# A wait ahead of the first weight load, finer evictions of one block, and an adapter product moved two matmuls ahead, in a fused low-rank-adapter and FFN kernel

## Chip, core and metric

The kernel runs on one core of one Trainium2 chip. The metric is device time in microseconds (us). TensorE is called PE, its weight load PEld, VectorE DVE, ScalarE ACT, GpSimd POOL, and SyncE SP; SP issues most of the DMAs. Code lines are written L424.

## What is computed

The input x has 8 sequences of 256 tokens and 1024 features. Each sequence picks one of 8 adapters of rank 16; the result goes through a gated FFN whose three inputs are rounded to fp8, and is added to x:

```
Bx   = einsum('bni,bri->bnr', x, B[ids])        # rank 16
c    = einsum('bnr,bor->bno', Bx, A[ids])       # 1024 features
q(v) = clip(v / in_scale, -448, 448) to fp8, times in_scale
h    = silu(q(c) @ gate.T) * (q(c) @ up.T)      # 2752 features
out  = x + q(h) @ down.T
```

## The kernel before

All tensors are held transposed: features on the 128 partitions, tokens along the free dimension. The 2048 tokens are four **blocks** t of 512 (two sequences each), the 1024 features eight pieces k of 128, and the 2752 hidden features 22 **chunks** c of 128 (the last has 64). One product is a 128x128 weight tile (bf16, the upper halves of f32 words) times a 128x512 tile of fp8 activations.

*Block 0.* SP loads block 0 of x in four pieces (`PIECES`, L46: k 0 to 1, 2 to 4, 5 to 6, 7; L432, L433, L441, L442), the adapters' B (`b_two`) and A (`a_two`), and then the gate and up weights of chunks 0 to 4 (`load_gate_up`, L418; 1 MB a chunk; chunks 0 and 1 in two halves; L445, L446). All these stand in one SP queue in program order. PE first runs 16 products of ones (`warm`, L750) that only pass time, then `two_times_b` (L553): the tile `bx`, B times x, over k 0 to 7, with two more passing products after k 6. DVE and ACT copy `bx` to `bm`; after six more passing products, `two_times_a` (L618) multiplies by A into `c` tiles, and `round_two` (L610) evicts them: scaled, rounded to fp8, into `xg[0]`, half on DVE (L606) and half on ACT (L608). Each eviction takes one k (256 columns, "singly") or two (512 columns).

*Chunks.* `gate_up(c, t)` (L677) makes 16 products, a gate sum over eight k and an up sum over eight k; `turns` tells in which order the two sums alternate, and `between` runs a function ahead of a given step. Then ACT does the silu (L695) and DVE multiplies and rounds into `hid` (L724). `wpool` holds five weight chunks, so chunk 5's load waits until PE is done with chunk 0. Instructions marked `keep_in_program_order` and all products stay in the order of the code.

*Block 1.* Block 0 runs through chunks 0 to 6 (`NHELD` is 7). Inside chunk 6, ahead of step 4, `two_times_b_in_parts` (L577) makes block 1's `bx`; ahead of step 10, `two_times_a_part(…, 0)` (L654) makes k 0 to 3 of `xg[1]`; and inside chunk 2 of block 1 (L794), ahead of step 5, `two_times_a_part(…, 1)` makes k 4 to 7. Block 1's x (`xs[1]`, 1.75 MB and 0.25 MB) is loaded by SP between the two halves of chunk 6's weights (L770). POOL doubles and splits the adapters for it, after its 1x1 copy at L756, which waits for chunk 2's weights.

*Blocks 2 and 3.* After chunks 3 and 4 of block 1, `four_times_b` (L797) makes `bx` for both blocks. Four groups of A follow, two k each (`four_times_a`, L667; 0 to 3): one inside chunk 5 of block 1, one after it, one inside chunk 6 ahead of step 8, one after it (L798 to L801). Each group has 16 products into four `c` tiles, then two evictions on ACT and two on DVE. Then blocks 2 and 3 pass chunks 2 to 6, and all blocks the rest; the down product (`yd`) and the addition of x (L847) end the kernel.

Of the kernel before, what the change touches and what calls it, by code (L numbers as in the profile page):

```python
# [34 lines left out]
NAHEAD = 2  # L35
NHELD = NFIRST + NAHEAD
# [17 lines left out]
def rows_of(c):  # L54
    return TAIL if c == NI - 1 else P


def high(ap):

    return ap.bitcast(BF16)[..., 1::2]  # L60
# [34 lines left out]
def gate_up_of(w_gu, c):  # L95
    at = c * 2 * NH * P * P
    return w_gu[at : at + 2 * NH * P * rows_of(c)].rearrange("(p n) -> p n", p=P)
# [204 lines left out]
def adaln_ffn(  # L302
# [15 lines left out]
    nc = tc.nc  # L318
# [45 lines left out]
    with ExitStack() as fast:  # L364
# [5 lines left out]
        xs = [acts.tile([P, NH, TB], F32, name=f"x{t}") for t in range(NTB)]  # L370
# [17 lines left out]
        def adapter_of(batch, queue):  # L388
            return queue.value_load(ids_i[0:1, batch : batch + 1], min_val=0, max_val=7)
# [25 lines left out]

        w_of = {}

        def load_gate_up(c, parts=1, between=()):  # L418
            n = NH if c == NI - 1 else 2 * NH
            w = wpool.tile([P, 2 * NH, P], F32, tag="w", name="w_gu")[:, :n]  # L420
            src = gate_up_of(w_gu, c).rearrange("p (k n) -> p k n", n=P)
            n //= parts
            for i in range(parts):
                nc.sync.dma_start(out=w[:, bass.ts(i, n)], in_=src[:, bass.ts(i, n)])  # L424
                if i == 0:
                    for load in between:
                        load()
            w_of[c] = w
# [14 lines left out]
        load_a_two(1, second)  # L443
        load_a_two(0, adapter_of(0, nc.sync))
        for c in range(NFIRST):  # L445
            load_gate_up(c, parts=2 if c < 2 else 1)  # L446
        adapters = [adapter_of(2 + q, nc.gpsimd if q < 2 else nc.sync) for q in range(6)]
        lane = const.tile([P, 1], I32, name="lane")
        nc.gpsimd.iota(lane, pattern=[[0, 1]], base=0, channel_multiplier=1)
# [153 lines left out]
        def round_to(to, c, engine):  # L603
            scale = inv[:, GATE_IN : GATE_IN + 1]
            if engine is nc.vector:
                nc.vector.tensor_scalar(to, c, scale, None, ALU.mult, saturate=False)  # L606
            else:
                nc.scalar.activation(to, c, AF.Copy, scale=scale, saturate=False)  # L608

        def round_two(t, part, cs, cut=False):  # L610
            for g in range(2):
                n = 1 if cut and g == 0 else 2
                for i, j in product(range(0, 2, n), range(2)):
                    k = KS * part + 2 * g + i
                    to = xg[t][:, k : k + n, bass.ts(j, SEQ)]
                    round_to(to, cs[2 * g + j][:, i : i + n], nc.vector if j else nc.scalar)

        def two_times_a(bm):  # L618


            n = SEQ // 2
            for part in range(2):
                cs = [psum.tile([P, 2, SEQ], F32, tag="ps", name=f"c{q}") for q in range(4)]
                for other, i in product(range(2), range(2)):
                    for q in (0, 2, 1, 3):
                        rows = slice(32 * q, 32 * (q + 1))
                        multiply(
                            cs[q][:, i, bass.ts(q % 2 ^ other, n)],
                            lhsT=a_two[0][rows, bass.ts(2 * part + i, P)],
                            rhs=bm[rows, other],  # L630
                            start=True,
                            stop=True,
                        )
                cs = [cs[2 * j + g] for g in range(2) for j in range(2)]
                round_two(0, part, cs, cut=part == 0)

        def times_a_parts(bms, a, at):

            cs = [psum.tile([P, 2, SEQ], F32, tag="ps", name=f"c{q}") for q in range(4)]
            for bm, i in product(bms, range(2)):
                for q in range(4):
                    rows = slice(32 * q, 32 * (q + 1))
                    multiply(
                        cs[q][:, i],
                        lhsT=a[rows, bass.ts(at + i, P)],
                        rhs=bm[rows],
                        start=bm is bms[0] and i == 0,
                        stop=bm is bms[-1] and i == 1,  # L650
                    )
            return cs

        def two_times_a_part(bms, part):  # L654
            round_two(1, part, times_a_parts(bms, a_parts[0], 2 * part), cut=True)

        def four_times_b():
            quads = [(q, 0, 2 + q // 2, bass.ts(q % 2, SEQ)) for q in range(4)]
# [8 lines left out]
        def four_times_a(bms, i):  # L667
            cs = times_a_parts(bms, a_parts[1 + i // 2], 2 * (i % 2))
            for q in range(4):
                to = xg[2 + q // 2][:, 2 * i : 2 * i + 2, bass.ts(q % 2, SEQ)]  # L670
                round_to(to, cs[q], nc.vector if q % 2 else nc.scalar)
# [5 lines left out]
        def gate_up(c, t, turns=(NH,), between={}):  # L677


            tail = c == NI - 1  # L680
            w = w_of[c]
            cols = bass.ts(t, TB)
            js = range(1 if tail else 2)
            ys = []
            steps = []
            for i, n in enumerate(turns):
                done = sum(turns[:i])
                steps += product(js, range(done, done + n))
            rows = slice(TAIL, P) if tail else slice(0, P)
            g = work.tile([P, TB], F32, tag="g", name="g")  # L690

            def silu():
                gates = ys[0][:TAIL] if tail else ys[0]
                early(
                    nc.scalar.activation(  # L695
                        g[rows], gates, AF.Silu, scale=gate_s[: gates.shape[0]]
                    )
                )

            def early(instruction):  # L700
                if c < NHELD:
                    tc.keep_in_program_order(instruction)

            for i, (j, k) in enumerate(steps):
                if i in between:
                    between[i]()
                if j == len(ys):
                    ys.append(psum.tile([P, TB], F32, tag="ps", name=f"y{j}"))
                multiply(
                    ys[j],  # L710
                    lhsT=high(w[:, row_of(c, j, k), :]),
                    rhs=xg[t][:, k, :],
                    start=(k == 0),
                    stop=(k == NH - 1),
                )
                if j == 0 and k == NH - 1:
                    silu()
            ups = ys[0][TAIL:] if tail else ys[1]
            if tail:
                to = lora.tile([P, 2 * TB], FP8, tag="bm", name="tail", bufs=2)[half_of(t), :TB]  # L720
            else:
                to = hid_of(c)[:, cols]
            early(
                nc.vector.scalar_tensor_tensor(  # L724
                    to,
                    in0=ups,
                    scalar=up_by_down[rows],
                    in1=g[rows],
                    op0=ALU.mult,
                    op1=ALU.mult,  # L730
                    saturate=False,
                )
            )
            if tail:
                nc.vector.tensor_copy(hid_tail[half_of(t), t // 2], to)
            if t == (NTB - 1 if NAHEAD <= c < NHELD else 2 if c < NAHEAD else 1):
                note_low_bits(w_of[c], P, c)
                if 1 < c <= 1 + 2 * NTB:
                    i, half = divmod(c - 2, 2)
                    ks = slice(half * NH // 2, (half + 1) * NH // 2)  # L740
                    note_squares(xg[i][:, ks, :], P, c - 2)
                before = NHELD - 1 if c == 0 else NAHEAD - 1 if c == NHELD else c - 1
                if c != NAHEAD:
                    note_squares(hid[before], P, 2 * NTB + before)
# [14 lines left out]
        for g, j in product(range(2), range(2)):  # L759
            load_a_twice(a_two[1], 2 * g + j, a8_twice, adapters[j] * 2 + g, nc.gpsimd)  # L760
        a_parts = [
            in_place_of_hid(NI - 8 - i, [P, H // 2], F32R, f"a_parts{i}") for i in range(3)
        ]
# [19 lines left out]
        for c in range(2, NHELD - 1):  # L783
            gate_up(c, 0)
        bms = []
# [3 lines left out]
            between={  # L789
                4: lambda: bms.append(two_times_b_in_parts()),  # L790
                10: lambda: two_times_a_part(bms[0], 0),
            },
        )
        gate_up(NAHEAD, 1, turns=(4, 1, 1, 2), between={5: lambda: two_times_a_part(bms[0], 1)})  # L794
        for c in range(NAHEAD + 1, NHELD - 2):
            gate_up(c, 1)
        bms.append(four_times_b())  # L797
        gate_up(NHELD - 2, 1, between={8: lambda: four_times_a(bms[1], 0)})  # L798
        four_times_a(bms[1], 1)
        gate_up(NHELD - 1, 1, between={8: lambda: four_times_a(bms[1], 2)})  # L800
        four_times_a(bms[1], 3)  # L801
        for c in range(NAHEAD, NHELD):
            for t in (2, 3):
                gate_up(c, t)
# [131 lines left out]
    with found_others.Else():  # L936

        k = NH - 1
        cut = TB - P
# [8 lines left out]
        t, cols = NTB - 1, slice(cut, TB)  # L948
# [91 lines left out]
```

## Time and profile before

| | |
|---|---|
| three timed runs | 474.25, 474.61 (median), 475.7 us |
| the profiled execution's own time | 474.17 us |
| its span (first to last instruction of the core) | 472.5 us |
| PE busy in the span | 468.6 us, 99% |
| ACT / DVE / POOL busy | 194.7 / 106.4 / 16.0 us |
| DMA, first four fortieths of the span | 304, 421, 377, 363 GB/s |
| DMA, mean over the span | 119 GB/s |

The profiled execution's time is 1.67 us more than its span; that lies around the span and is taken as unchanged. A PE that is "busy" can still be short of its full pace, because matmuls are pipelined and the recorded 0.379 us of a 512-column product reaches into the next ones; what counts is the distance between the starts of two products, 0.216 us where nothing holds them. The profile shows which engine sat idle before an instruction and what ended the wait, and of each DMA the time from its issue to its landing.

### The profile page before, as it was taken

Reading aid. Unit: us, or ns where it says so; the run is one execution under the profiler, and the core shown is the slowest. Engines: PE = TensorE matmul, PEld = TensorE weight load, DVE = VectorE, ACT = ScalarE, POOL = GpSimd, SP = SyncE. Lnnn points to the kernel's source line nnn. Section 1 sums busy time; section 2 is a strip of 40 time slices with the busy share of each in tenths; the row PEclk is TensorE's granted clock in tenths of the full one; section 3 lists DMA queues with packets and bytes.
Section 4 is the critical chain, followed back from the end, with each engine's and each line's share of the span. In section 5 each row is a group of like instructions: output and inputs, shape, how many; then the busy total and the mean of one; then the engine's idle time right before and its main releaser. Section 6 shows DMA issues by size and latency. Waiting matters only on the chain.

```text
span 472.5 us, 5982 instructions
## 1 busy us (share of the span) xinstructions
PE 468.6 (99%) x2479; PEld 214.7 (45%) x2479; DVE 106.4 (23%) x169; ACT 194.7 (41%) x256; POOL 16.0 (3%) x32
## 2 busy tenths in 40 slices
PE   9999999999999999999999999999999999999997
PEld 5454444444444444444444444444444444444444
DVE  1314351222121221212122121231120111031031
ACT  2315258996655655453345545359112012021000
POOL 0230500000000000000000000000000000000000
PEclk9999999999999999999999999999999999999999
DMA  8999104352222211222220011132435245163031
GB/s 304 421 377 363 47 3 154 115 177 89 90 89 90 86 24 69 89 90 89 90 84 21 30 62 57 61 113 95 131 120 161 81 170 162 38 209 104 5 114 68
DMA packets 14661, 56.01 MB, mean 119 GB/s; under 512 B 1762, under 2 KB 2786, under 8 KB 12066
## 3 DMA queue, kind: packets, MB, share of 16 engines
q1 hardware_dynamic: 14256, 55.08, 34.0%
q8 instruction: 21, 0.34, 0.3%
q0 software_dynamic: 192, 0.40, 0.3%
q14 instruction: 14, 0.11, 0.1%
q10 hardware_dynamic: 178, 0.07, 0.1%
HBM read 47.15 MB, written 8.39 MB: 118 GB/s over the span
## 4 chain that ended last, share of the span: by engine, by line
PE 99%; DVE 0%; issue 0%
PE y L521 63%; PE yd L521 32%; PE bx L521 2%; PE warm L521 2%; PE c L521 1%; DVE o L847 0%; PE count L521 0%
## 5 line engine op out<-in xcount | busy, mean ns | idle before, releaser
L521 PE MATMUL y<-xg,w_gu 128*128 128x512 fp8e4 x1376 | 298.9, 379 | 0.0
L521 PEld LDWEIGHTS <-w_gu 128*128 128x128 bf16 x1376 | 133.5, 98 | 162.5 <-DVE xg L606 2.1
L521 PE MATMUL yd<-hid,w_d 128*128 128x512 fp8e4 (+2 forms) x693 | 146.0, 373 | 0.0
L695 ACT ACTIVATE g<-y,gate_s 128x512 f32<-128x512 f32 (+1 forms) x88 | 59.5, 681 | 134.2 <-PE y L521 134.1
L724 DVE SCALAR_TENSOR_TENSOR hid<-y,up_by_down,g 128x512 fp8e4<-128x512 f32 x84 | 63.1, 751 | 216.9 <-PE y L521 146.4
L521 PEld LDWEIGHTS <-w_d 128*128 128x128 bf16 x693 | 66.6, 98 | 79.0 <-issue 1.7
L507 ACT ACTIVATE junk<-w_d 128x1408 bf16<-128x1408 uint16 (+1 forms) x16 | 21.2, 1324 | 88.3 <-DMA w_d<-w_d 88.2
L847 DVE SCALAR_TENSOR_TENSOR o<-yd,down_s,x 128x512 f32<-128x512 f32 x28 | 20.0, 748 | 107.4 <-PE yd L521 92.8
L507 ACT ACTIVATE junk<-w_gu 128x2048 bf16<-128x2048 uint16 (+1 forms) x22 | 41.0, 1864 | 0.0
L514 ACT ACTIVATE junk<-hid 128x2048 bf16<-128x2048 fp8e4 x21 | 40.1, 1908 | 0.6
L514 ACT ACTIVATE junk<-xg 128x2048 bf16<-128x2048 fp8e4 x8 | 15.3, 1911 | 0.3
L606 DVE TENSOR_SCALAR xg<-c,inv 128x512 fp8e4<-128x512 f32 (+1 forms) x19 | 11.5, 660 | 5.6 <-PE c L521 5.6
L608 ACT ACTIVATE xg<-c,inv 128x512 fp8e4<-128x512 f32 (+1 forms) x19 | 10.4, 618 | 4.9 <-PE c L521 4.9
L521 PE MATMUL warm<-const-bfloat16-1.0 128*128 128x512 bf16 (+1 forms) x24 | 7.3, 470 | 0.9 <-PEq L1029 0.9
L847 DVE SCALAR_TENSOR_TENSOR o<-yd,down_s,xg 128x512 f32<-128x512 f32 (+2 forms) x5 | 3.2, 644 | 12.4 <-PE yd L521 12.4
L521 PEld LDWEIGHTS <-const-bfloat16-1.0 128*128 128x128 bf16 x25 | 2.7, 124 | 5.3 <-issue 5.2
L507 ACT ACTIVATION_READ_ACCUMULATOR junk<-w_gu 128x1 f32 x22 | 4.2, 193 | 0.0
L521 PE MATMUL yd<-hid_tail,w_dt 64*128 64x512 bf16 (+1 forms) x32 | 4.2, 377 | 0.0
L724 DVE SCALAR_TENSOR_TENSOR tail<-y,up_by_down,g 64x512 fp8e4<-64x512 f32 x4 | 3.0, 757 | 4.9 <-ACT g L695 4.8
L514 ACT ACTIVATION_READ_ACCUMULATOR junk<-hid 128x1 f32 x21 | 3.9, 187 | 0.0
L521 PE MATMUL bx<-x,b_four_twice 128*32 128x256 f32 x64 | 3.7, 380 | 0.0
L460 POOL TENSOR_SCALAR a_parts<-a_four,minus 128x512 fp32r<-128x512 f32 x2 | 3.1, 1562 | 1.2 <-DMA a_four<-a_twice 1.2
(69 smaller groups left out, 55.1 us busy)
## 6 DMA issues: line engine op xcount, KB each, us to landing
w_gu<-w_gu SPq DMA_DIRECT2D x17, 1024.0 KB, 5.0
outT<-o SPq DMA_DIRECT2D x31, 256.0 KB, 2.1
w_gu<-w_gu SPq DMA_DIRECT2D x13, 512.0 KB, 5.7
w_d<-w_d SPq DMA_DIRECT2D x8, 704.0 KB, 5.2
w_d<-w_d SPq DMA_DIRECT2D x8, 640.0 KB, 3.9
x<-x SPq DMA_DIRECT2D x2, 2048.0 KB, 19.9
x<-x SPq DMA_DIRECT2D x1, 1792.0 KB, 14.1
x<-x SPq DMA_DIRECT2D x2, 512.0 KB, 3.9
```

The costliest lines, as they stand in the source:

```text
L460: held(engine.tensor_scalar(parts, a, minus, None, ALU.mult))
L507: nc.scalar.activation(junk_like(w), low(w), AF.Copy, accum_out=lows[:rows, column : column + 1])
L514: nc.scalar.activation(junk_like(q), q, AF.Square, accum_out=squares[:rows, column : column + 1])
L521: tc.keep_in_program_order(nc.tensor.matmul(*args, **kwargs))
L606: nc.vector.tensor_scalar(to, c, scale, None, ALU.mult, saturate=False)
L608: nc.scalar.activation(to, c, AF.Copy, scale=scale, saturate=False)
L695: nc.scalar.activation(g[rows], gates, AF.Silu, scale=gate_s[: gates.shape[0]])
L724: nc.vector.scalar_tensor_tensor(to, in0=ups, scalar=up_by_down[rows], in1=g[rows], op0=ALU.mult, op1=ALU.mult, saturate=False,)
L847: nc.vector.scalar_tensor_tensor(o, in0=y, scalar=down_s, in1=x, op0=ALU.mult, op1=ALU.add)
```

## The change

Four edits.

1. `load_gate_up` takes an optional `behind`: DVE copies one element of it into the weight tile before the load is issued, so the load waits for that copy, and the copy for the DMA that brings `behind`. For chunk 0, `behind` is one element of k 5 of block 0's x, which lands with k 6.
2. `round_two`'s `cut` becomes the number of groups (0, 1 or 2) that are evicted singly. Block 0's two parts stay as they were (1 and 0), block 1's part 0 too (1); block 1's part 1 goes from one group to both, so that k 6 and k 7 are evicted singly as well.
3. The order of the sums in chunk 2 of block 1 goes from `(4, 1, 1, 2)` to `(4, 1, 1, 1, 1)`: gate 6, up 6, gate 7, up 7 instead of gate 6, gate 7, up 6, up 7.
4. The last group of A for blocks 2 and 3 is placed ahead of step 14 of chunk 6 of block 1, instead of behind step 15.

```diff
-        def load_gate_up(c, parts=1, between=()):
+        def load_gate_up(c, parts=1, between=(), behind=None):
             n = NH if c == NI - 1 else 2 * NH
             w = wpool.tile([P, 2 * NH, P], F32, tag="w", name="w_gu")[:, :n]
+            if behind is not None:
+                nc.vector.tensor_copy(w[:1, 0, :1], behind)
...
         for c in range(NFIRST):
-            load_gate_up(c, parts=2 if c < 2 else 1)
+            load_gate_up(c, parts=2 if c < 2 else 1, behind=None if c else xs[0][:1, 5, :1])
...
-        def round_two(t, part, cs, cut=False):
+        def round_two(t, part, cs, cut=0):
             for g in range(2):
-                n = 1 if cut and g == 0 else 2
+                n = 1 if g < cut else 2
...
-                round_two(0, part, cs, cut=part == 0)
+                round_two(0, part, cs, cut=1 - part)
...
-            round_two(1, part, times_a_parts(bms, a_parts[0], 2 * part), cut=True)
+            round_two(1, part, times_a_parts(bms, a_parts[0], 2 * part), cut=1 + part)
...
-        gate_up(NAHEAD, 1, turns=(4, 1, 1, 2), between={5: lambda: two_times_a_part(bms[0], 1)})
+        gate_up(NAHEAD, 1, turns=(4, 1, 1, 1, 1), between={5: lambda: two_times_a_part(bms[0], 1)})
...
-        gate_up(NHELD - 1, 1, between={8: lambda: four_times_a(bms[1], 2)})
-        four_times_a(bms[1], 3)
+        gate_up(
+            NHELD - 1,
+            1,
+            between={
+                8: lambda: four_times_a(bms[1], 2),
+                14: lambda: four_times_a(bms[1], 3),
+            },
+        )
```

## The prediction

> **What bounds the kernel now.** I read the page's busy times and its chain first, to see which engine sets the end.
>
> ```profile
> PE 468.6 (99%) x2479; PEld 214.7 (45%) x2479; DVE 106.4 (23%) x169; ACT 194.7 (41%) x256; POOL 16.0 (3%) x32
> ...
> PE 99%; DVE 0%; issue 0%
> PE y L521 63%; PE yd L521 32%; PE bx L521 2%; PE warm L521 2%; PE c L521 1%; DVE o L847 0%; PE count L521 0%
> ```
>
> The chain is PE from end to end: whatever delays one product delays the end, and only time taken out of PE's own sequence is gained. Next, the starts of successive products. From 12.19 to 33.57 us, and from 65.9 us to the down stage, they stand 0.216 us apart with nothing between, so no stall there can be removed. What other engines add shows as idle time of the weight loads (PEld, last bracket of a timeline row):
>
> ```profile
> 12.19 21.76 PE L521 MATMUL y<-xg,w_gu 128*128 128x512 fp8e4 x100
> 33.88 0.72 PEld L521 LDWEIGHTS bx<-x,b_twice 128*32 128x32 f32 x28 [0.42 <-issue]
> 42.74 0.76 PEld L521 LDWEIGHTS <-w_gu 128*128 128x128 bf16 x5 [0.50 <-DVE xg L606]
> 65.64 0.76 PEld L521 LDWEIGHTS <-w_gu 128*128 128x128 bf16 x5 [0.41 <-DVE xg L606]
> ```
>
> The reader is to see two waits for an eviction (42.74, 65.64), and that `bx` of block 1 at 33.88 shows the same 0.42 as the tile switches at 7.34 (0.43), 37.19 and 50.62: it waits for no data, so far. Third, the DMAs, by stretches (share of the 16 engines and GB/s last) and by single issues (last number: us to landing; issued at 3.46, 6.18, 8.08 and 19.68):
>
> ```profile
> 7.20:8.30 1.10, 1.10 (x37) 0.96 (x40) 0.01 (x1) 0.00 (x0) 0.00 (x0) 1.00 1.01 380
> 8.30:9.50 1.20, 1.20 (x40) 0.78 (x30) 0.00 (x0) 0.00 (x0) 0.00 (x0) 1.00 1.08 270
> 14.00:19.00 5.00, 5.00 (x25) 2.29 (x24) 0.96 (x2) 1.37 (x2) 0.18 (x1) 1.00 1.01 421
> 28.50:34.00 5.50, 5.50 (x30) 2.35 (x31) 1.50 (x2) 0.82 (x2) 2.83 (x2) 1.00 1.02 417
> ```
> ```profile
> x<-x SPq DMA_DIRECT2D x1, 512.0 KB, 4.5
> w_gu<-w_gu SPq DMA_DIRECT2D x1, 512.0 KB, 5.0
> w_gu<-w_gu SPq DMA_DIRECT2D x1, 1024.0 KB, 10.4
> x<-x SPq DMA_DIRECT2D x1, 1792.0 KB, 14.1
> ```
>
> The DMA engines are full from about 3 to 44 us. Loads land in the order of issue, so each is as late as all before it. PE and DMA run neck and neck: chunk 0's first half lands at 6.18 + 5.0 = 11.2 and is used at 12.19 (cover 1.0); chunk 2 lands at 8.08 + 10.4 = 18.5, used at 19.11 (0.6); block 1's x lands at 19.68 + 14.1 = 33.8, and its `bx` starts at 33.88 (0.1 at most, 0.05 when PE's 0.06 from a signal to its start is counted: an eviction ends at 41.63, its weight load starts at 41.69).
>
> **Edit 1, the wait ahead of chunk 0.** k 5 and 6 land at 3.46 + 4.5 = 7.92 (more exactly than the row). DVE is idle from 7.21 to 9.69, so the copy starts at 7.95 (B's landing at 6.42 starts L477 at 6.45), takes 0.15 (a 128x1 operation here) and reaches SP 0.05 later: the issue moves from 6.18 to 8.15. Behind the waiting issue SP holds the other six weight loads of L446, four reads of adapter numbers, chunks 5 and 6 and the x of blocks 1 to 3; ACT's and POOL's queues don't move, but POOL's copy at L756 waits for chunk 2, and its loads with it.
>
> The issue is 1.97 late, yet in before the load queued behind x and A until about 8.3. What a 512 KB load takes on a queue that is empty, the trace shows: 3.3 (x, at 0.86), 3.9 (weights, at 86.36 and 100.58), 5.6 (weights, at 93.47). Landing is then 8.15 + 3.3 = 11.45, 12.05 or 13.75 against 11.2, a delay D of 0.25, 0.85 or 2.55. Below, D could be 0, if the 270 GB/s of 8.3 to 9.5 are a start-up that is then hidden behind k 7 and A; less is excluded, since a load that is issued later, in the same order, does not land sooner. I take D = 0.6, between the two rows that lie nearest: k 7 and A are still moving until 8.9, so the engines don't start from rest as at 86.36. All later loads land D later (a full queue gives nothing back), until the DMA has room after 44. The starts of PE follow by the largest of D − 1.0 (chunk 0), D − 0.6 (chunk 2), D − 0.05 (block 1's x): **+0.55**. Nothing more comes later: POOL's doubled B of blocks 2 and 3 is ready at 49.2, used at 50.62, its split A at 53.4 and 56.25, used at 56.04 and 61.06, and PE is late by nearly as much as they are.
>
> Does block 0 gain? Its `bx` uses k 5 at 8.6 (landed 7.92) and k 7 at 9.22 (landed 8.9), and `c` starts at 10.07 (A landed 9.7), right after the copies of `bm` begin to end at 9.97. PE waits for none of these loads, so a sooner landing is worth nothing.
>
> The Trainium skill (DMA: Bandwidth & Descriptors, "Rules for kernel authors") speaks against this edit: issue the DMA early and wait for it late. The 0.1 of cover at 33.8 says the same here. Its "Specifications" give 0.6 us to the first byte for loads issued by SP; the trace has about 0.9 (issued at 0.86, first bytes in the slice from 1.75). By the page's figure D would be some 0.3 less, and the total about 474.6.
>
> **Edits 2 and 3, k 6 and k 7 of block 1.** The product at 42.74 starts 0.391 after the one before, instead of 0.216, and the next loses another 0.012: 0.19 in all. It waits for the 512-column eviction, which DVE ends at 42.68 (start 41.94, 0.741). Singly, k 6 takes 41.94 to 42.42 (0.48, as at 41.15) and k 7 starts 0.40 later and ends at 42.82. Gate 6 is due at 42.57 and has its data at 42.42 + 0.06 = 42.48; up 6 follows at 42.78; gate 7 is due at 43.00 and has its data at 42.88. So the stall goes: **−0.19**. The price, one eviction more on ACT and DVE and 0.14 more for k 7, lies in idle time (ACT's next work comes at 43.39, DVE's at 44.11). If k 7 ended 0.12 later than this, that much would come back. Interleaving the sums costs PE nothing: both orders hold the same 16 products.
>
> **Edit 4, the last group of A two products sooner.** At 65.64 the start is 0.299 after the one before: 0.083, and 0.011 at the next. DVE evicts k 6 and 7 of block 2 from 64.84 to 65.59, because it first did chunk 6's `hid` (64.18, 0.75). Two steps sooner, `c` starts at 63.14 instead of 63.57, DVE evicts from 63.98 (0.84 after the start, as at 58.55 and 59.40) to 64.72 for block 2 and to 65.38 for block 3, ahead of `hid`. k 6 of block 2 is due at 65.56: **−0.09**. The tile switches stay two. The four `c` tiles need a bank that ACT frees at 62.53, 0.6 before. `hid` ends at about 66.1, 1.1 later; who needs it or its bank is the up sum of block 3, at about 69.4, so this is covered.
>
> **The sum.** 0.55 − 0.19 − 0.09 = +0.27 against the profiled execution's 474.17 (span 472.5 and 1.67 around it): 474.44. The median of the timed runs stands 0.44 above that execution, and I carry that over: **474.9**.
>
> **The rivals.**
> *A slow restart of the load (slower).* One mechanism: the first weights, issued to a queue that has run dry, take what the 512 KB at 93.47 took, 5.6. D is 2.55, PE stalls 1.5 at chunk 0 and at `bx` of block 1 2.5 in all: 474.61 + 2.5 − 0.28 = 476.8. It decides, for my bound of 0.3%, from D = 1.8 on. For it: a load on an idle queue is slow at its start (at 72.41, 1 MB took 4.9, where 421 GB/s would make 2.5). Against it: other loads are still moving until 8.9. Chance 0.2.
> *The wait is hidden (D = 0 to 0.1).* Then only the stalls go: 474.61 − 0.28 = 474.3. For it: the old load also moved slowly at 8.3 to 9.5. This is within the same class as the forecast.
> *Sooner x and A help.* If the weights in the queue had slowed them, and the timed runs more than the profiled one, `c` could start at most 0.33 sooner (A at 9.7 against 10.07), with 0.44 of the median and 0.28 of stalls: 473.6. Even that is under 0.3%. For more, a cause that this trace does not show is needed: 0.06.
> *The finer eviction doesn't do what it says.* If k 7 is late by more than its 0.12, the stall only moves, and 0.19 of the gain is lost: 475.1.
>
> **How the numbers follow.** 0.3% of 474.61 is 1.4 us, about what a measurement of this kernel can tell from no change. The forecast, with the hidden wait and the moved stall beside it, lies within it: 0.74. Slower by more has the slow restart's 0.2, faster by more 0.06. The range runs from the hidden wait, less 0.3 of the spread of the timed runs, 474.0, to 476.6, near the end of the slow restart.
>
> **What would show it.** In the new profile: the first weight issue at about 8.15 and its landing at 11.4 to 12.1; block 1's x landing at about 34.4; PEld idle by more than 0.42 ahead of block 1's `bx`, and perhaps ahead of chunk 2; the waits for L606's evictions gone at block 1's k 6 and at block 2's k 6. I am wrong if `bx` of block 1 still starts at 33.9 with 0.42 (D is hidden), if the first landing is past 13 (restart), or if an idle time stands before gate 7.

## The result, and the profile after

| | before | after |
|---|---|---|
| median of 14 runs each, us | 474.37 (474.11 to 475.7) | 475.12 (474.89 to 476.4) |
| profiled execution, us (span) | 474.17 (472.5) | 474.89 (473.2) |
| ratio of the runs, 95% interval | | 1.0017 [1.001, 1.0024] |

The changed kernel is 0.75 us slower. The interval does not hold 1, so the loss is clear of the noise, but it is inside the 0.3% that the prediction counted as the same. Busy times and chain on the page of the changed kernel:

```profile
PE 468.3 (99%) x2479; PEld 214.5 (45%) x2479; DVE 106.7 (23%) x171; ACT 194.8 (41%) x257; POOL 16.0 (3%) x32
...
PE 93%; DMA 6%; SPq 0%; issue 0%; DVE 0%
PE y L523 59%; PE yd L523 32%; DMA x<-x 4%; DMA w_gu<-w_gu 1%; PE bx L523 1%; PE c L523 1%; DMA ids_i<-ids 0%; SPq L426 0%; SPq L389 0%; SPq L392 0%; DVE o L855 0%; DVE w_gu L422 0%; PE count L523 0%
```

DVE has two instructions more (the copy, one eviction), ACT one. PE's busy time is 0.3 us *less*, yet the kernel is longer. The chain tells why: it is no longer PE alone. It runs back from the end through PE to `bx` of block 1, there to the DMA that brings block 1's x (`x<-x`, 4%), and further back over 16 products, the weight load that they waited for and L426's issues to the copy at L422. So the start of the chain has moved from PE to the load queue.

The stretches of the changed kernel, cut as in the prediction, with one more, 9.5 to 12 us (share of the 16 DMA engines and GB/s are last):

```profile
7.20:8.30 1.10, 1.10 (x48) 0.95 (x40) 0.15 (x2) 0.00 (x0) 0.00 (x0) 1.00 1.02 391
8.30:9.50 1.20, 1.17 (x24) 0.62 (x16) 0.28 (x1) 0.24 (x1) 0.00 (x0) 1.00 0.67 111
9.50:12.00 2.50, 2.31 (x67) 2.03 (x64) 1.64 (x5) 1.75 (x6) 0.00 (x0) 1.00 0.92 293
14.00:19.00 5.00, 4.90 (x24) 2.04 (x23) 0.75 (x1) 1.37 (x2) 0.00 (x0) 1.00 1.01 410
28.50:34.00 5.50, 5.50 (x28) 2.45 (x25) 1.13 (x2) 1.24 (x2) 2.83 (x2) 1.00 0.99 390
```

The stretch that the prediction does not show, in the kernel before:

```profile
9.50:12.00 2.50, 2.50 (x78) 2.31 (x70) 1.48 (x5) 1.54 (x6) 0.00 (x0) 1.00 1.02 393
```

From 8.3 to 9.5 us the engines move 111 GB/s (270 before), and from 9.5 to 12 293 GB/s (393 before). From the start to 12 us, 3246 KB (of 1000 bytes) have been moved instead of 3664: 418 KB less. At 33 us it is 11539 KB instead of 11934, 395 KB less. What was lost by 12 us was never made up, and 400 KB at the 421 GB/s of the full queue are 0.95 us.

The weight loads and `bx` of block 1, in the timelines of PEld and of PE of the changed kernel:

```profile
12.20 3.14 PEld L523 LDWEIGHTS <-w_gu 128*128 128x128 bf16 x16 [0.58 <-DMA w_gu<-w_gu]
15.93 3.14 PEld L523 LDWEIGHTS <-w_gu 128*128 128x128 bf16 x16 [0.59 <-DMA w_gu<-w_gu]
19.52 14.36 PEld L523 LDWEIGHTS <-w_gu 128*128 128x128 bf16 x68 [0.45 <-DMA w_gu<-w_gu]
34.76 1.72 PEld L523 LDWEIGHTS bx<-x,b_twice 128*32 128x32 f32 x64 [0.88 <-issue]
...
42.58 0.12 PEld L523 LDWEIGHTS <-w_gu 128*128 128x128 bf16 x2 [0.34 <-DVE xg L608]
42.97 0.15 PEld L523 LDWEIGHTS <-w_gu 128*128 128x128 bf16 x2 [0.28 <-DVE xg L608]
43.37 0.19 PEld L523 LDWEIGHTS <-w_gu 128*128 128x128 bf16 x2 [0.24 <-DVE xg L608]
43.76 7.14 PEld L523 LDWEIGHTS <-w_gu 128*128 128x128 bf16 x34 [0.20 <-DVE xg L608]
...
64.52 2.49 PEld L523 LDWEIGHTS <-w_gu 128*128 128x128 bf16 x13
```
```profile
34.79 1.47 PE L523 MATMUL bx<-x,b_twice 128*32 128x128 f32 x45 [0.42 <-DMA x<-x]
```

Three waits for weights now stand in block 0, at the starts of chunks 0, 1 and 2. Ahead of `bx` of block 1 PEld is idle for 0.88 instead of 0.42, and PE's own row names the DMA of x. On PEld the same wait is put down to "issue": one reads both engines' rows before calling a gap a plain tile switch. The wait of 0.50 at block 1's k 6 and the one of 0.41 at block 2's k 6 are gone; in place of the first, four short idle times of 0.34 to 0.20 stand, at which PE loses nothing (its starts stay 0.215 to 0.234 apart).

### The profile page after: what moved, and what is told of

Same layout as the page of the kernel before. It is cut to its first block, busy times and chain, and to the rows that moved or that the text cites. A ratio compares the mean times of both kernels' runs of the same rounds, so it can differ in the third digit from the quotient of the medians.

```text
span 473.2 us, 5986 instructions
## 1 busy us (share of the span) xinstructions
PE 468.3 (99%) x2479; PEld 214.5 (45%) x2479; DVE 106.7 (23%) x171; ACT 194.8 (41%) x257; POOL 16.0 (3%) x32
## 4 chain that ended last, share of the span: by engine, by line
PE 93%; DMA 6%; SPq 0%; issue 0%; DVE 0%
PE y L523 59%; PE yd L523 32%; DMA x<-x 4%; DMA w_gu<-w_gu 1%; PE bx L523 1%; PE c L523 1%; DMA ids_i<-ids 0%; SPq L426 0%; SPq L389 0%; SPq L392 0%; DVE o L855 0%; DVE w_gu L422 0%; PE count L523 0%
```

## The experiments

**My theory** after the result: block 1's x sets the time. `bx` of block 1 starts 0.13 to 0.15 us after that load has landed on the last of the 16 DMA engines; what follows is fixed work for PE. The wait ahead of chunk 0 lets the load queue run dry, and every load behind it is late by what the engines did not move. **Rivals:** the wait itself is harmless and only the empty time costs (then an earlier or filled wait is free); POOL's small loads collide with the later stream; the 0.75 comes from edits 2 to 4, or they bring nothing. All diffs are against the changed kernel. "To the last product" is the time from the start of `bx` of block 1 to PE's last start, which holds all that happens later.

| kernel | first weight issue | chunk 0's half lands | block 1's x lands | `bx` starts | to the last product | median (before in the same comparison) |
|---|---|---|---|---|---|---|
| before | 6.18 | 11.21 | 33.77 | 33.90 | 435.43 | 474.37 |
| before, run again | 6.19 | 11.18 | 33.64 | 33.79 | 435.43 | one run, 474.06 |
| after | 8.00 | 12.16 | 34.66 | 34.79 | 435.15 | 475.12 (474.37) |
| after, run again | 8.00 | 12.15 | 34.71 | 34.84 | 435.15 | one run, 474.91 (474.13) |
| edit 1 alone | 8.06 | 12.09 | 34.50 | 34.64 | 435.33 | 475.61 (474.37) |
| edits 2 to 4 | 6.19 | 11.16 | 33.84 | 33.98 | 435.12 | 474.37 (474.37) |
| edits 2 and 3 | 6.23 | 11.51 | 33.51 | 33.64 | 435.16 | one run, 473.67 |
| copy waits for k 2 | 7.01 | 11.69 | 34.18 | 34.32 | 435.13 | 474.91 (474.37) |
| the same, run again | 7.15 | 11.41 | 34.76 | 34.90 | 435.16 | one run, 474.98 (474.13) |
| copy waits for k 7 | 9.04 | 13.02 | 35.61 | 35.74 | 435.14 | 476.08 (474.37) |
| copy ahead of chunk 1 | 6.27 | 11.37 | 33.60 | 33.75 | 435.14 | 474.31 (474.31) |

Executions differ too: the five of this table with a first issue at 6.2 to 6.3 have block 1's x between 33.51 and 33.84.

**Edit 1 alone.** Edits 2 to 4 are as in the kernel before:

```diff
-                n = 1 if g < cut else 2
+                n = 1 if cut and g == 0 else 2
-            round_two(1, part, times_a_parts(bms, a_parts[0], 2 * part), cut=1 + part)
+            round_two(1, part, times_a_parts(bms, a_parts[0], 2 * part), cut=True)
-        gate_up(NAHEAD, 1, turns=(4, 1, 1, 1, 1), between={5: lambda: two_times_a_part(bms[0], 1)})
+        gate_up(NAHEAD, 1, turns=(4, 1, 1, 2), between={5: lambda: two_times_a_part(bms[0], 1)})
-                14: lambda: four_times_a(bms[1], 3),
+        four_times_a(bms[1], 3)
```

> Edit 1 alone on the kernel before: only the wait ahead of chunk 0's load. Theory (the wait lets the DMA queue run dry; what lands late is block 1's x): the first weight issue at 8.0, chunk 0's first half landed at 12.2 instead of 11.2, block 1's bx at about 34.8 instead of 33.9, time +0.9 to +1.0 us against before (more than the changed kernel's +0.75, because the two stalls at k 6 are still there). Rival A (the eviction and reordering edits cost the 0.75, the wait is hidden): 0.0 +- 0.1. Rival B (the waiting DVE copy and its signal cost by themselves, whatever it waits for): about +0.9 as well; another kernel of this call tells it from the theory.

Measured: 475.61, ratio 1.0024 [1.0015, 1.0033]; the profiled execution took 474.92. The whole loss is in edit 1. In the timeline of its PEld the old wait at k 6 stands again, 0.73 later than in the kernel before, but the one at block 2's k 6 does not, although edit 4 is undone:

```profile
43.47 7.45 PEld L523 LDWEIGHTS <-w_gu 128*128 128x128 bf16 x36 [0.50 <-DVE xg L608]
...
64.98 2.06 PEld L523 LDWEIGHTS <-w_gu 128*128 128x128 bf16 x11
```

So what removed that second wait is not the move of the product; see below.

**Edits 2 to 4 without the wait.**

```diff
-            load_gate_up(c, parts=2 if c < 2 else 1, behind=None if c else xs[0][:1, 5, :1])
+            load_gate_up(c, parts=2 if c < 2 else 1)
```

> The changed kernel without edit 1: finer evictions, interleaved sums and the earlier last group of A alone. Theory: the first weight issue back at 6.2, block 1's bx at 33.9 with 0.42 of idle weight loads ahead of it, no wait for an eviction at k 6, time -0.25 to -0.3 us against before, faster than both kernels. Rival A: +0.75. Rival C (the stalls taken out are given back later, to a wait for the x of blocks 2 and 3): 0.0.

Measured: 474.37 against 474.37, ratio 0.9996 [0.9987, 1.0005]. The trace shows 435.12 instead of 435.43 behind `bx`, 0.31 gained, which is too little for the timed runs to tell from nothing. In this execution block 1's x happened to land 0.08 later than before.

**The wait moved earlier: the copy reads k 2**, which lands 1.7 us before k 5 (6.17 and 7.82 in this run). The copy does not start there: it stands behind six operations of DVE that wait for B, starts at 6.84, and the first weights are issued at 7.01, 1.0 sooner than in the changed kernel.

```diff
-            load_gate_up(c, parts=2 if c < 2 else 1, behind=None if c else xs[0][:1, 5, :1])
+            load_gate_up(c, parts=2 if c < 2 else 1, behind=None if c else xs[0][:1, 2, :1])
```

> The changed kernel with the copy waiting for k 2 of block 0's x (landed at 6.15) instead of k 5. The copy, its signal and SP's wait are all still there. Theory: the issue comes at about 7.1 to 7.4, while k 7 and A are still moving until 8.5, and with 0.9 from issue to first byte the queue is empty for 0.1 at most: between -0.3 and 0.0 us against before. Rival B: +0.75, as the changed kernel.

Measured: 474.91, ratio 1.0011 [1.0002, 1.002]. This went against the theory of an empty queue alone: other loads keep the engines at work until the weights come, and block 1's x is still 0.41 late.

**The wait moved later: the copy reads k 7.**

```diff
-            load_gate_up(c, parts=2 if c < 2 else 1, behind=None if c else xs[0][:1, 5, :1])
+            load_gate_up(c, parts=2 if c < 2 else 1, behind=None if c else xs[0][:1, 7, :1])
```

> The changed kernel with the copy waiting for k 7 of block 0's x (landed at 8.7 to 8.9). Theory: the issue comes at about 9.0, 1.0 later than in the changed kernel, on a queue that is empty; all landings and block 1's bx are 0.9 to 1.1 later than there: +1.6 to +1.9 us against before. Rival B: +0.75, no more than the changed kernel.

Measured: 476.08, ratio 1.0038 [1.0024, 1.0052]. The issue at 9.04 finds an empty queue, and the loss grows with the delay. The stretches of this kernel:

```profile
8.30:9.50 1.20, 1.07 (x27) 0.53 (x16) 0.29 (x2) 0.09 (x1) 0.00 (x0) 1.00 0.21 55
9.50:12.00 2.50, 2.44 (x69) 2.14 (x66) 1.65 (x6) 1.79 (x6) 0.00 (x0) 1.00 0.64 169
```

55 and 169 GB/s, where the kernel before has 270 and 393: (215 x 1.2 + 224 x 2.5) / 421 is an estimate of 1.9 us, and block 1's x lands 1.84 later.

**The gap filled.** k 7 of block 1's x (256 KB) is loaded ahead of the waiting issue.

```diff
+        load_x(1, NH - 1)
         for c in range(NFIRST):
             load_gate_up(c, parts=2 if c < 2 else 1, behind=None if c else xs[0][:1, 5, :1])
...
-            NHELD - 1, parts=2, between=(lambda: load_x(1, 0), lambda: load_x(1, NH - 1))
+            NHELD - 1, parts=2, between=(lambda: load_x(1, 0),)
```

> The changed kernel with the 256 KB of k 7 of block 1's x loaded ahead of the gated weight load (behind A) instead of behind the rest of block 1's x. The wait and its issue at 8.0 stay; the queue that runs dry at 8.6 now has 0.6 us more to move, and the same bytes are before block 1's x. Theory (what is lost is the time in which the queue is empty and restarts): block 1's x lands at 34.0 to 34.3 instead of 34.7, time +0.2 to +0.4 us against before. Rival B' (the lateness of the issue itself is what costs, whatever is moved meanwhile): +0.75, as the changed kernel.

Measured: 475.37, ratio 1.0018 [1.0008, 1.0029]: no better than the changed kernel. One slip of mine is in it: the 256 KB now stand ahead of the other seven eighths of block 1's x, so those land 0.6 us later for that alone (256 KB at 421 GB/s). All of block 1's x is there at 35.11, against 34.41 for k 7 in the kernel before: 0.70 late, where the changed kernel has 35.34, 0.93 late. Filling the gap gave back 0.22. The stretches of this kernel show where the rest stayed:

```profile
8.30:9.50 1.20, 1.07 (x26) 0.50 (x15) 0.12 (x1) 0.07 (x1) 0.00 (x0) 1.00 1.08 270
9.50:12.00 2.50, 2.40 (x70) 2.15 (x67) 1.53 (x6) 1.65 (x6) 0.00 (x0) 1.00 1.00 288
```

The first is as good as before (270), the second is not (288 against 393), at a DMA share of 1.00. The engines are at work, but their packets take longer: from 10 to 11 us the packets of 4096 bytes take 0.35 us each in the mean, where they take 0.16 from 12 us on.

**The copy ahead of chunk 1.** Chunk 0 is issued as before; the other five weight loads wait for k 5.

```diff
-            load_gate_up(c, parts=2 if c < 2 else 1, behind=None if c else xs[0][:1, 5, :1])
+            load_gate_up(c, parts=2 if c < 2 else 1, behind=xs[0][:1, 5, :1] if c == 1 else None)
```

> The changed kernel with the same copy (k 5 of block 0's x) put into chunk 1's tile instead of chunk 0's: chunk 0's two halves are issued at 6.2 and 6.7 as in the kernel before, the five loads from chunk 1 on at 8.0 and later as in the changed kernel, but behind 1 MB that is still to move. Theory (what costs is that the weight stream starts late, on a queue that has run down; a late issue on a full queue costs nothing): chunk 0 lands at 11.2, block 1's x at 33.6 to 33.9, its bx at 33.8 to 34.0, -0.2 to -0.3 us against before, faster than or equal to the kernel without any wait. Rival B (the wait, the copy or the lateness of the later issues costs by itself): +0.5 to +0.75.

Measured: 474.31 against 474.31, ratio 0.9998 [0.9989, 1.0007]. The same wait, with the same copy, costs nothing when 1 MB stands in the queue ahead of it. PEld in this kernel:

```profile
12.82 20.50 PEld L523 LDWEIGHTS <-w_gu 128*128 128x128 bf16 x96 [0.22 <-DVE xg L608]
33.74 1.69 PEld L523 LDWEIGHTS bx<-x,b_twice 128*32 128x32 f32 x64 [0.42 <-issue]
```

96 weight loads without an idle time, and the plain 0.42 at `bx`. This experiment, with the changed kernel beside it, puts the cost on the late issue of chunk 0, and clears the copy, the semaphore and the late issue of the later chunks.

**POOL's loads.** Two kernels let SP issue the six loads that POOL issues, with the wait (as shown) and without it (also without `behind`), because the load rate drops to 334 GB/s between 23 and 28.5 us in the kernel before, while those loads run.

```diff
-        adapters = [adapter_of(2 + q, nc.gpsimd if q < 2 else nc.sync) for q in range(6)]
+        adapters = [adapter_of(2 + q, nc.sync) for q in range(6)]
...
-        tc.keep_in_program_order(nc.gpsimd.tensor_copy(b_two[1][:1, :1], w_of[2][:1, 0, :1]))
...
-            load_b(b_two[1], j, adapters[j], nc.gpsimd)
+            load_b(b_two[1], j, adapters[j], nc.sync)
-            load_a_twice(a_two[1], 2 * g + j, a8_twice, adapters[j] * 2 + g, nc.gpsimd)
+            load_a_twice(a_two[1], 2 * g + j, a8_twice, adapters[j] * 2 + g, nc.sync)
```

> The changed kernel with the six small adapter loads for block 1 issued by SP, in its queue behind chunk 5, instead of by POOL, and without POOL's 1x1 copy that holds them back. In the trace the DMA moves 334 GB/s from 23 to 28.5 us, while POOL's loads are in flight, against 420 before and after. Theory (block 1's x is the landing that PE waits for): it lands 0.5 to 1.0 sooner, the wait ahead of block 1's bx goes, what stays is PE's lateness of 0.4 from chunks 0 to 2: +0.2 to +0.4 us against before. Rival D (the loss is paid at chunks 0 to 2, or the slow stretch has another cause than POOL's loads): +0.75.

> The same SP loads without edit 1: candidate for the fastest version. Theory: no wait ahead of block 1's bx, 0.1 less than the kernel with edits 2 to 4 alone; -0.3 to -0.4 us against before. Rival D: -0.2 or slower.

Measured: 475.63, ratio 1.0022 [1.001, 1.0034], and 474.55, ratio 1.0005 [0.9987, 1.0024]. Both expectations of a gain missed. The rate from 23 to 28.5 us is 331 and 279 GB/s, so POOL's loads were not what held it down, and the move has a price of its own: on SP each DMA waited for the landing of the one eight places back (27.49 with the wait), so block 1's x was issued at 27.51 instead of 19.97 with the wait, and at 26.65 instead of 19.70 without it. It landed at 34.91 and 34.21. (These two traces begin 0.13 us later in the program: the first load is issued at 0.73 in them, at 0.86 in the others.) The rival falls; the dip itself stays unexplained.

**Before, run again**, to see whether the late start of one DVE instruction at 64.18 was chance.

```diff
-            load_gate_up(c, parts=2 if c < 2 else 1, behind=None if c else xs[0][:1, 5, :1])
+            load_gate_up(c, parts=2 if c < 2 else 1)
...
-        gate_up(NAHEAD, 1, turns=(4, 1, 1, 1, 1), between={5: lambda: two_times_a_part(bms[0], 1)})
+        gate_up(NAHEAD, 1, turns=(4, 1, 1, 2), between={5: lambda: two_times_a_part(bms[0], 1)})
```

(and the other edits undone, so that this is the kernel before)

> The kernel before once more, for a second look at the stall of 0.083 us ahead of block 2's k 6, which edit 4 was credited with. In the profile before, DVE's hid of chunk 6 started 0.91 after the last product of its sum; elsewhere it is 0.49. Theory (that was one late start of DVE in one execution, and edit 4 removes nothing that is there in general): hid starts 0.49 after, no stall at block 2's k 6. Rival (the stall belongs to the order of the work): 0.08 again. Block 1's k 6 shows its 0.39 either way, and the time is that of before.

Measured: the wait is there again. DVE and PEld in this second execution of the kernel before:

```profile
64.06 0.75 DVE L724 SCALAR_TENSOR_TENSOR hid<-y,up_by_down,g 128x512 fp8e4<-128x512 f32 x1 [0.90 <-PE y L521]
64.73 1.40 DVE L606 TENSOR_SCALAR xg<-c,inv 128x512 fp8e4<-128x512 f32 x2
```
```profile
65.53 1.41 PEld L521 LDWEIGHTS <-w_gu 128*128 128x128 bf16 x8 [0.41 <-DVE xg L606]
```

What `hid` waits for was there at 63.55; it started 0.52 later, where the `hid` before it (58.62) started 0.09 later. So this is no chance of one execution.

**Edits 2 and 3 alone**, to see whether that late start sits at one place of DVE's program.

```diff
-            load_gate_up(c, parts=2 if c < 2 else 1, behind=None if c else xs[0][:1, 5, :1])
+            load_gate_up(c, parts=2 if c < 2 else 1)
...
-                14: lambda: four_times_a(bms[1], 3),
+        four_times_a(bms[1], 3)
```

> Edits 2 and 3 alone on the kernel before: k 6 and 7 of block 1 evicted singly and the sums interleaved; no wait ahead of chunk 0, the last group of A where it was. From the start of block 1's bx to PE's last product it is 435.43 us in both profiles of the kernel before and 435.12 to 435.15 with edits 2 to 4. Theory (the 0.08 at block 2's k 6 came of a late start of DVE's hid, 0.47 after its signal, that sits at one place of DVE's program and moves when an instruction is added ahead of it): no stall there even without edit 4, 435.13 to 435.16. Rival (edit 4 takes the 0.09 away): a stall of 0.08 at block 2's k 6, 435.23 to 435.26.

Measured: 473.67 in one run. One eviction more on DVE, and `hid` starts 0.48 after the work before it, not 0.90 (0.10 after its data, not 0.52); no weight load waits at block 2's k 6, without edit 4. DVE and PEld of this kernel:

```profile
63.33 0.75 DVE L724 SCALAR_TENSOR_TENSOR hid<-y,up_by_down,g 128x512 fp8e4<-128x512 f32 x1 [0.48 <-PE y L521]
```
```profile
63.81 3.14 PEld L521 LDWEIGHTS <-w_gu 128*128 128x128 bf16 x16
```

**The wait for k 2 and the changed kernel, run again.** The kernels are unchanged.

```diff
-            load_gate_up(c, parts=2 if c < 2 else 1, behind=None if c else xs[0][:1, 5, :1])
+            load_gate_up(c, parts=2 if c < 2 else 1, behind=None if c else xs[0][:1, 2, :1])
```

> The kernel whose copy waits for k 2 once more, for a second look at its landings: in the first profile its weight stream began as early as in the kernel before (first bytes at 8.3), and yet block 1's x landed 0.3 to 0.5 later (34.18), because the last of the 16 engines brought chunk 0's first half 1.1 after the first one, against 0.5 to 0.6 elsewhere. If that belongs to the later issue, x lands at 34.1 to 34.3 again; if it was chance in one execution, at 33.6 to 33.9. Either way block 1's bx starts 0.13 to 0.15 after that landing or at PE's own pace, whichever is later.

> The changed kernel once more, for a second look at the delay: theory: first weight issue at 8.0 to 8.1, block 1's x landed at 34.5 to 34.7, its bx 0.13 later, 435.14 us from there to PE's last product. Rival (the landing varies by as much as the delay itself from one execution to the next): x landed below 34.2 or above 35.0.

Measured: one run each, 474.98 and 474.91, with 474.13 for the kernel before. The changed kernel repeats itself (block 1's x at 34.71, before it 34.66). The wait for k 2 does not: 34.76 in this execution, 34.18 in the first. Its stretches:

```profile
9.50:12.00 2.50, 2.50 (x74) 2.35 (x70) 1.52 (x5) 1.59 (x6) 0.00 (x0) 1.00 0.92 323
12.00:14.00 2.00, 2.00 (x16) 0.83 (x12) 2.00 (x4) 1.76 (x4) 0.00 (x0) 1.00 1.06 332
```

Besides the slower stretch up to 12 us (323 GB/s, 393 before), this execution moves 332 GB/s from 12 to 14 us, where the kernel before has 426. In the second of the two, the last of the 16 engines was already 1.9 us behind the first when the second weight load landed, at 13.85. So, counted from the 33.77 of the kernel before, an issue at 7.1 loses 0.4 to 1.0 us, an issue at 8.0 0.7 to 0.9, one at 9.0 1.8.

## Why the prediction was right, and where it was off

The forecast was 474.9, inside 0.3% and on the slower side; the median is 475.12.

1. *The first issue at 8.15.* It came at 8.00. The copy started at 7.83, not 7.95. The changed kernel's DVE:

```profile
7.83 0.14 DVE L422 COPY w_gu<-x 1x1 f32<-1x1 f32 x1 [0.61 <-DMA x<-x]
```

2. *D = 0.6, taken between the bounds 0 and 2.55.* This is the mis-sized term. Chunk 0's first half landed at 12.16, D = 0.95; block 1's x at 34.66, D = 0.89. Three executions of the changed kernel and of edit 1 alone give 0.73 to 0.94 for the latter. I had argued down from the row of 0.85 because k 7 and A "are still moving until 8.9". They were, but too little: 111 GB/s from 8.3 to 9.5. And the filled queue still began its weights slowly, so that what is moving ahead helped by only 0.22.
3. *A full queue gives nothing back.* Right: 418 KB behind at 12 us, 395 KB at 33 us.
4. *PE follows by the largest of three differences.* Right in its form, but the cover of 0.05 at block 1's x was not there. `bx` started 0.89 later, by all of D. In the ten traces in which `bx` stands 0.385 us or more behind the product ahead of it, it starts 0.135 to 0.136 us after x has landed, and in the kernel before it is 0.136 already: there PE's last product of block 0 starts 0.331 before `bx`, where 0.309 is the plain distance at the tile switch of 50.62. So the kernel before waited for x too, by 0.02. Chunks 0 to 2 waited as well, but all of that is swallowed at block 1's x: whatever PE loses earlier, it would have waited there.
5. *PE waits for none of block 0's loads, so sooner x is worth nothing.* The reason is wrong, the value right. The last twelve of the 16 products of ones before `bx` take 4.85 us in the traced execution of before and 4.25 and 3.87 in those of the changed kernel and of edits 2 to 4; where they end sooner, PE does wait for k 7 (0.36 on PE's row at 9.23 of edits 2 to 4). A sooner x then lets `c` start sooner, at 9.63 instead of 10.07 in the changed kernel, but PE stands at 12.2 again, for chunk 0.
6. *Edits 2 and 3, −0.19.* Right. From `bx` to the last product it is 435.33 with edit 1 alone and 435.15 with all: 0.18 to 0.19.
7. *Edit 4, −0.09.* The 0.09 is gained, but already without edit 4, which ran nowhere alone. The late start of `hid`, which I took for the order of DVE's work, hangs on the place in DVE's program: with one DVE instruction added ahead of it (the copy of edit 1, or the eviction of edit 2) this `hid` starts on time. With that, edit 4 has nothing left to win. What causes the late start is not settled, but the traces hold a hint. In them 12 `hid` start 0.41 to 0.52 us after the last thing that they wait for; each time, 0.67 to 0.69 us after the start, the profile has one DMA packet of 8192 bytes of the kind "instruction". The DMA queues of the kernel before from 64.8 to 65.2 us, with this packet alone:

```profile
q14 instruction: 1, 0.01, 5.1%
```

That DVE stands still there for its own next instructions fits, but is not shown.
8. *The 0.44 from the profiled execution to the median.* Too much. Over 14 runs the medians stand 0.20 and 0.23 above the profiled executions; three runs were too few. Nor is this distance a constant: in the other kernels with several timed runs it lies between 0.06 and 0.69.

Together: 474.17 + 0.89 − 0.28 gives 474.78, 0.11 less than the changed kernel's own profiled time (0.08 of the rest lies behind PE's last product), and 0.23 to the median. The term for block 1's x was 0.34 too small (D by 0.29, and the cover of 0.05), and the carry 0.21 too large. That the forecast came within 0.22 of the median is in part luck: the two misses have opposite signs.

Of the rivals, the slow restart had the right mechanism and a wrong size (0.9, not 2.5); the hidden wait, sooner x and A as a gain, and a failing finer eviction fell. The Trainium skill's advice to issue a DMA early and wait late (DMA: Bandwidth & Descriptors, "Rules for kernel authors") agrees with the row of medians: 474.37 for an issue at 6.2, 474.91 at 7.0, 475.12 at 8.0, 476.08 at 9.0. With 1 MB ahead of them, the later five loads could be issued 0.5 to 1.0 us later than before at no cost that 11 runs show.

No kernel here measurably beats the one before. Edits 2 to 4 and the copy ahead of chunk 1 have shorter profiled spans (472.3 and 472.1 against 472.5) but the same medians. The one run of edits 2 and 3, 473.67, lies below the lowest of 15 runs of the kernel before (473.99); in it PE began chunk 0 at 11.96 instead of 12.19 and block 1's x landed 0.26 sooner, and one run can't tell the edits from such chance.

## What to carry to other kernels

Before a load is made to wait, find the next place at which PE has no cover against that load *queue*, not against that load: here the price of a late first weight was paid 22 us later, at block 1's x. Ask how many bytes stand in the queue ahead of the delayed issue; with 1 MB a late issue was free, with about 1 us' worth of bytes (the filled gap) or less it was not. And where a stall follows a late start on another engine, undo the edit that is to remove it: each of two other edits removed this one.

## What the runs showed of the hardware

- *The first weights come slowly even with loads ahead of them.* With the issue 2.1 us ahead of the time when the queue reaches it (before), the slow start lies in 8.3 to 9.5 us; with some 1.2 to 1.7 us of lead (k 2, filled gap) the stretch to 12 us is slow as well, 288 to 324 GB/s instead of 393. That the lead is the cause fits all rows, but no run varied the lead alone, so it is argued and not shown; nor is it known why the wait for k 2 lost 0.4 in one execution and 1.0 in the other. On a queue that had run nearly dry, the first packet of the weights came 0.99 to 1.01 us after the issue (8.00 to 8.99 in the changed kernel, 9.04 to 10.04 with k 7).
- *A load is as late as its slowest engine.* The landing of chunk 0's half spreads over 0.4 to 1.1 us from the first of the 16 engines to the last, that of block 1's x over 1.5 (33.17 to 34.66 in the changed kernel), 1.9 in the second execution of the wait for k 2, and 2.1 with the filled gap. The Trainium skill says that the 16 engines finish independently and that the semaphore counts them (DMA: Bandwidth & Descriptors, "Why a DMA increments its semaphore by 16 and not by 1"); the rows agree, and show that the wait ends with the last. In the kernel before the spread is 0.5 to 0.6 for the weight loads landed by 13.72 and 1.5 for the next ones (16.00, 18.49); between them, at 13.79, the profile has one packet of 16384 bytes of the kind "instruction" that took 1.03 us. It may have held up one engine; the trace does not say on which engine a packet ran, so what sets the spread stays open.
- *A DVE instruction can start some 0.5 us after its data*, at the same place of the program in each execution of one kernel (64.18 and 64.06 in the kernel before, the same again at 282.54 and 282.43 with 0.41), and no longer there when one DVE instruction is added. With two added, another `hid` is late (279.69 in the changed kernel, by 0.45).
- *The products of ones differ from execution to execution*: 12 of them took 3.87 to 4.85 us. In every trace they start about 0.43 us apart at first and 0.22 apart from a point on that lies between 4.7 and 6.8 us, at a granted clock of 1.00 in all the stretches.
